# A split-precision self-attention block: exponentials stationary in groups of 256 queries, changed to v stationary with 512 queries streamed

## The chip, the cores and the metric

The kernel runs on one core of a Trainium2 chip. The metric is the device time of one execution in microseconds, the median of several runs. Engines are named as the profile names them: PE is TensorE (its weight loads are PEld), DVE is VectorE, ACT is ScalarE, POOL is GpSimd, SP is SyncE. POOL and SP also issue DMAs here, each in the order of its own queue.

## What is computed

```python
# x (4, 64, 64, 256), Wq and Wk (256, 128), Wv (256, 256); N = 64 * 64 = 4096
q = einsum('bwhc,cd->bwhd', x, Wq) + bq
k = einsum('bwhc,cd->bwhd', x, Wk) + bk
v = einsum('bwhc,cd->bwhd', x, Wv) + bv
pq, pk, pv = (t.reshape(B, -1, N) for t in (q, k, v))     # (4, 128, N), (4, 128, N), (4, 256, N)
energy = einsum('bcn,bcm->bnm', pq, pk)                   # (4, N, N)
attention = softmax(energy, axis=-1)
out = einsum('bcm,bnm->bcn', pv, attention).reshape(x.shape)
return gamma * out + x
```

The reshape is not a transpose: the flat memory of q is read anew as 128 rows of 4096. For each of the four images, 4096 queries n meet 4096 keys m; the weights are normalised over the keys, and 256 rows of v are summed with them.

## The kernel before

**Three forms of each operand.** The matrix unit is fed in a shorter float type (fp32r). To keep float32 accuracy, each operand is split into a rounded upper part h, a remainder l and a combination d, and a product of two float32 matrices is made of three products of forms: h by h and l by l into one accumulator, d by d into another or ahead of the two. For the energies, the product of the third forms comes first (`cross`, products at L322), ScalarE scales it in place in PSUM (L337), the products of the other two forms are added (`energy`, L322 too), and ScalarE takes the exponential (L347). Of each tile of exponentials x, ScalarE makes h (`upper`, L356), and VectorE makes l (L362) and d (L365) (`halves`).

**Tiling.** 128 partitions hold keys. An image has 16 groups of NB = 256 queries, and a group has NU = 8 steps of four key tiles of 128. So an image has 128 steps. In a step, `cross` and `energy` make 12 products with k's form stationary and q's form moving 256 columns, each pair of key tiles in one of four PSUM banks named e. `attend` (L405) makes 24 products with the *exponentials'* forms stationary (128 keys by 128 queries) and v's forms moving: into banks a0 and a1 (one for each half of the group's queries) 258 columns, 256 of v and two of ones, which give the sums of the exponentials, and into bank bb 256 columns for d. The order of a step's 24 products is written out (`ORDERS`). Cross runs four steps ahead of attend, energy three.

**Group end.** At a group's last step ScalarE copies a0 and a1 out (L417). `finish` then runs in pieces, one piece at each call of `proceed`, over the next steps: VectorE copies the two sums (L423), takes the reciprocal (L425), multiplies by gamma (L426) and adds bb (L427); ScalarE scales by the reciprocal (L430); TensorE transposes the result (four products, L438, into bank t); VectorE adds x (L442), which SP loaded three steps before the group's end; POOL's queue stores 256 KB (L443). The last group of all goes through `finish_last` (L450 to L487). All sums are kept on the chip and tested once, at the very end, against the range in which the short path is valid; outside it a general path would run, which does not happen with this data.

**Projection.** Before an image's steps, 16 iterations i (with `begin` interleaving the first energies of the image from i = 10 on) load x (L82, SP's queue), transpose it (L122, copied by L128), and make q and k (`qk`, eight records of float32 products at L135, bias by VectorE at L144) and v (L156, bias by ScalarE at L165). `project_qk` stores q as it is (two DMAs of 64 KB, L275) and k's three forms (384 KB, L279) in HBM, on POOL's queue; k's forms are made by L263 (ScalarE) and L266 (VectorE) in a tile f with two buffers. v's forms stay on the chip (`halve_v`, L292 and L296).

**What sets the order.** The schedule is manual: instructions stand on each engine's queue in the order in which the program issues them, and tiles' buffers make the waits. A step of the main loop issues cross, energy with exponential, `load_k` (all three forms of four key tiles, 768 KB, L314, on POOL's queue; three buffers) for the cross of the next step, halves of the next step, then attend. `load_q` (L303, SP's queue) brings q's values once a group, and `halve_q` makes its forms. POOL's queue therefore holds k's loads and the output's stores, SP's holds x and q.

Of the kernel before, what the change touches and what calls it, by code (L numbers as in the profile page):

```python
# [20 lines left out]
def kernel(  # L21
# [36 lines left out]
    nc = tc.nc  # L58
# [114 lines left out]
    NB = 256  # L173
    NJ = NB // P
    NG = N // NB
    NU = NM // 4
    STEPS = NG * NU
    LOOK = 3
    VC = C + 4
# [4 lines left out]

    again = const.tile([P, 1], I32, name="again")
    zs = const.tile([P, 1], F32, name="zs")

    zall = const.tile([P, B * NG, NJ], F32, name="zall")
# [10 lines left out]
    with ExitStack() as fast:  # L199
# [5 lines left out]

        pool("pad", 1).tile([P, 16], F32, name="pad")
        ppool = pool("ppool", 2)
        pool("pad2", 1).tile([P, 112], F32, name="pad2")
        work = pool("work", 2)
        pool("pad3", 1).tile([P, 48], F32, name="pad3")  # L210
        kpool = pool("kpool", 3)
        dram = pool("dram", 2, space=DRAM)
        ps_s = pool("ps_s", 4, space=PSUM)
        ps_o = pool("ps_o", 1, space=PSUM)
        ps_t = pool("ps_t", 1, space=PSUM)


        vh = qkv.tile([P, NM, VC], F32R, tag="vh", name="vh")
        vl = qkv.tile([P, NM, VC], F32R, tag="vl", name="vl")
        vd = qkv.tile([P, NM, C], F32R, tag="vd", name="vd")  # L220
        for t in (vh, vl):
            nc.scalar.copy(t[:, :, C : C + 2], ones[:, : 2 * NM].rearrange("p (m t) -> p m t", t=2))
# [5 lines left out]
        energies = cycle([(ps_s, "e")])  # L228
        outputs = cycle([(ps_o, "a0"), (ps_o, "a1"), (ps_o, "bb"), (ps_t, "t")])
# [11 lines left out]
        def image(b):  # L241
# [13 lines left out]
            for g in range(NG):  # L255
                qd[b, g] = dram.tile([P, NJ, P], F32, tag=f"qd{g}", name=f"qd_{b}_{g}")
            for t in range(NU):
                kf[b, t] = dram.tile([P, 2, 2, 3 * P], F32R, tag=f"kf{t}", name=f"kf_{b}_{t}")

        def halved(f, x):  # L260

            h = f[:, :, 0, :]
            nc.scalar.activation(h, x, AF.Identity, scale=UPPER / 64)  # L263
            yield
            for j, s, op in ((1, -64.0, ALU.add), (2, 64.0 * (1.0 + E), ALU.subtract)):
                nc.vector.scalar_tensor_tensor(  # L266
                    f[:, :, j, :], h.bitcast(F32), s, x, ALU.mult, op
                )
            yield

        def project_qk(b, i):
            images[b].qk(i)
            x = now["qk"]
            for s in range(2):
                nc.gpsimd.dma_start(qd[b, i // 2 + NG // 2 * s][:, i % 2, :], x[:, s, :C2])  # L275
            f = kpool.tile([P, 2, 3, P], F32R, tag="f", name=f"f_{b}_{i}", bufs=2)
            for _ in halved(f, x[:, :, C2:]):
                pass
            nc.gpsimd.dma_start(kf[b, i // 2][:, i % 2], f.rearrange("p s j d -> p s (j d)"))  # L279
# [8 lines left out]
        def halve_v(b, i):  # L288
            v4 = units.pop((b, "v4", i))
            m = slice(2 * i, 2 * i + 2)  # L290
            h = vh[:, m, :C]
            nc.scalar.activation(h, v4, AF.Identity, scale=UPPER * E)  # L292
            yield

            for t, f in ((vl, 1.0 / E), (vd, 1.0 / E + 1.0)):
                nc.vector.scalar_tensor_tensor(  # L296
                    t[:, m, :C], h.bitcast(F32), -f, v4, ALU.mult, ALU.add
                )
            yield

        def load_q(b, g):
            t = work.tile([P, NJ, P], F32, tag="qr", name=f"qr_{b}_{g}", bufs=1)
            nc.sync.dma_start(t, qd[b, g])  # L303
            loads[b, "qr", g] = t

        def halve_q(b, g):
            t = work.tile([P, 3, NJ, P], F32R, tag="q", name=f"q_{b}_{g}")
            loads[b, "q", g] = t
            yield from halved(t.rearrange("p f j d -> p j f d"), loads.pop((b, "qr", g)))

        def load_k(b, u):
            if u < STEPS:
                t = kpool.tile([P, 4, 3, P], F32R, tag="k", name=f"k_{b}_{u}")
                nc.gpsimd.dma_start(t.rearrange("p (i s) f d -> p i s (f d)", s=2), kf[b, u % NU])  # L314
                loads[b, "k", u] = t

        def chunk(b, u, k, f, first):

            g, t = divmod(u, NU)
            q, kt, e = loads[b, "q", g], loads[b, "k", u], units[b, "e", u, k]  # L320
            for i in range(2):
                nc.tensor.matmul(  # L322
                    e[:, i],
                    kt[:, 2 * k + i, f, :],
                    q[:, f],
                    start=first and i == 0,
                    stop=(f == 1),
                    skip_group_check=True,
                )

        def cross(b, u, k):
# [3 lines left out]
            e = units[b, "e", u, k] = ps_s.tile([P, 2, NJ, P], F32, tag="e", name=f"e_{b}_{u}_{k}")  # L335
            chunk(b, u, k, 2, True)
            nc.scalar.mul(e, e, -1.0 / (1.0 + E))  # L337

        def energy(b, u, k):
# [3 lines left out]
            for f in range(2):  # L343
                chunk(b, u, k, f, False)
            if k == 0:
                units[b, u] = ppool.tile([P, 4, NB], F32, tag="x", name=f"x_{b}_{u}", bufs=3)
            nc.scalar.activation(  # L347
                units[b, u][:, 2 * k : 2 * k + 2, :],
                units.pop((b, "e", u, k)).rearrange("p i j d -> p i (j d)"),
                AF.Exp,  # L350
                scale=(1.0 + E) / E,
            )

        def upper(b, u):
            h = ppool.tile([P, 4, NB], F32R, tag="h", name=f"h_{b}_{u}", bufs=3)
# [3 lines left out]
        def halves(b, u):  # L359
            x, h = units[b, u]  # L360
            l = ppool.tile([P, 4, NB], F32R, tag="l", name=f"l_{b}_{u}")
            nc.vector.tensor_tensor(l, x, h.bitcast(F32), ALU.subtract)  # L362

            d = ppool.tile([P, 4, NB], F32R, tag="d", name=f"d_{b}_{u}")
            nc.vector.scalar_tensor_tensor(  # L365
                d, h.bitcast(F32), 1.0 + E, x, ALU.mult, ALU.subtract
            )
            units[b, u] = h, l, d

        ORDERS = (
            ("13564072", "14325076"),
            ("41256307", "41763502"),
            ("26147053", "35601472"),
            ("41236075", "57104632"),
            ("10436572", "10726543"),
            ("57164203", "34250167"),
            ("35042176", "65341027"),
            ("35210467", "15347062"),  # L380
        )

        def order(f, b, g, t):
            return "01234567" if f == 2 else ORDERS[t][f]

        def attend(b, u):

            g, t = divmod(u, NU)
            if t == 0:
                now["acc"] = [  # L390
                    ps_o.tile([P, C + 2], F32, tag=f"a{j}", name=f"a{j}_{b}_{g}")
                    for j in range(NJ)
                ]
                now["bb"] = ps_o.tile([P, NJ, C], F32, tag="bb", name=f"bb_{b}_{g}")
            h, l, d = units[b, u]
            acc, bb = now["acc"], now["bb"]
            begun = set()
            for f, (left, right) in enumerate(((h, vh), (l, vl), (d, vd))):
                for n, x in enumerate(order(f, b, g, t)):
                    j, i = divmod(int(x), 4)  # L400
# [315 lines left out]
```

## Time and profile before

| what | value |
| --- | --- |
| runs shown, median of 3 | 2455.34 us (2453.41 to 2458.25) |
| profiled execution: its time / its span | 2454.75 us / 2452.9 us |
| granted clock of TensorE in that execution | 0.999 |
| DMA: bytes moved, mean rate | 498.92 MB, 203 GB/s |
| POOL's queue (q0): share of 16 DMA engines | 59.5% |
| chain that ended last: PE / DMA | 91% / 4% |
| products of the energies (L322), busy | 794.7 us in 6144 |
| products of attend (L405), busy, three groups | 569.7, 568.9 and 553.0 us in 4096 each |

The profile is of one execution; its span is the time between its first and last recorded instruction, 1.85 us less than the time of that execution. Busy time of an engine is the union of its instructions' times, so overlapping products do not add up. In the groups of instructions a row gives line, engine, operation, output and inputs (buffer numbers left out), shape, count, then busy time and mean duration of one, then the engine's idle time just before them with what ended most of it. Mean durations of pipelined products overlap (a product of 256 columns lasts 0.278 us, and the next starts 0.113 us after it), so that costs are read from distances of starts, not from durations. In a row of the windows stand: the window, its length, busy time and number of instructions of PE, PEld, DVE, ACT and POOL, the granted clock, the busy share of the DMA engines, and GB/s.

### The profile page before, as it was taken

What the parts mean: (1) busy time and instruction counts of PE and PEld (TensorE: products, weight loads), DVE (VectorE), ACT (ScalarE), POOL (GpSimd) and SP (SyncE); (2) the same over time, 40 slices, a digit from 0 to 9 for tenths busy, and PEclk for the clock granted to TensorE, in tenths of its full rate; (3) what the DMA queues carried; (4) which work ended last, traced back from release to release, by engine and by line L of the source; (5) the groups of instructions that cost most, each with busy time, mean ns of one, the idle gap of its engine ahead of it and who ended that gap; (6) DMA issues with size and microseconds to landing.
All of it is one profiled execution on the core that took longest, in us unless ns stands there. A gap on an engine that the chain in (4) does not pass through costs nothing.

```text
span 2452.9 us, 50094 instructions
## 1 busy us (share of the span) xinstructions
PE 2429.7 (99%) x19988; PEld 2394.9 (98%) x19988; DVE 1523.2 (62%) x1806; ACT 1799.7 (73%) x3201; POOL 424.3 (17%) x781
## 2 busy tenths in 40 slices
PE   9999999999999999999999999999999999999998
PEld 8999999999899999999989999999998999999998
DVE  5666666656665666666566666666566666666665
ACT  5777777777677777777667777777766777777775
POOL 4211111111411111111141111111114111111110
PEclk9999999999999999999999999999999999999999
DMA  7666666665766666666477666666647666666663
GB/s 234 207 207 207 205 211 198 211 207 162 235 204 204 207 207 211 203 203 209 149 241 216 203 205 212 204 212 202 206 146 245 212 207 203 208 205 203 209 205 114
DMA packets 137408, 498.92 MB, mean 203 GB/s; under 512 B 15536, under 2 KB 57264, under 8 KB 137168
## 3 DMA queue, kind: packets, MB, share of 16 engines
q0 software_dynamic: 92320, 453.17, 59.5%
q1 hardware_dynamic: 44304, 42.22, 5.5%
q8 instruction: 160, 2.62, 0.4%
q14 instruction: 80, 0.66, 0.1%
q10 hardware_dynamic: 544, 0.26, 0.0%
HBM read 445.25 MB, written 50.33 MB: 202 GB/s over the span
## 4 chain that ended last, share of the span: by engine, by line
PE 91%; DMA 4%; issue 2%; ACT 1%; DVE 1%; POOL 1%; SPq 0%; POOLq 0%; DVEq 0%; ACTq 0%
PE a L405 38%; PE e L322 28%; PE bb L405 18%; DMA k<-kf 3%; PE qk L135 3%; PE v L156 2%; PE ot L438 1%; DMA kf<-f 1%; PE xt L122 1%; ACT v L165 0%; DVE qks L144 0%; DVE f L266 0%; ACT f L263 0%; DMA x<-in_x_dram 0%; ACT vh L292 0%
## 5 line engine op out<-in xcount | busy, mean ns | idle before, releaser
L337 ACT ACTIVATE e<-e 128x512 f32<-128x512 f32 x1024 | 549.6, 580 | 507.7 <-PE e L322 507.6
L362 DVE TENSOR_TENSOR l<-x,h 128x1024 fp32r<-128x1024 f32 x512 | 626.2, 1223 | 452.1 <-ACT x L347 436.3
L322 PE MATMUL e<-q,k 128*128 128x256 f32 x6144 | 794.7, 278 | 11.6 <-DMA k<-kf 10.2
L322 PEld LDWEIGHTS e<-q,k 128*128 128x128 f32 x6144 | 738.7, 188 | 16.4 <-issue 11.0
L347 ACT ACTIVATE x<-e 128x512 f32<-128x512 f32 x1024 | 621.9, 608 | 5.5 <-issue 5.5
L365 DVE SCALAR_TENSOR_TENSOR d<-h,x 128x1024 fp32r<-128x1024 f32 x512 | 624.0, 1219 | 0.0
L405 PE MATMUL a<-vh,h 128*128 128x258 f32 x4096 | 569.7, 281 | 0.0
L405 PE MATMUL a<-vl,l 128*128 128x258 f32 x4096 | 568.9, 281 | 0.0
L405 PE MATMUL bb<-vd,d 128*128 128x256 f32 x4096 | 553.0, 277 | 0.0
L356 ACT ACTIVATE h<-x 128x1024 fp32r<-128x1024 f32 x512 | 548.4, 1071 | 0.1
L314 POOL DMA_DIRECT2D k<-kf x512 | 274.2, 535 | 1579.7 <-PE e L322 1554.6
L405 PEld LDWEIGHTS a<-vl,l 128*128 128x128 f32 x4096 | 522.0, 189 | 0.0
L405 PEld LDWEIGHTS a<-vh,h 128*128 128x128 f32 x4096 | 519.4, 189 | 0.0
L405 PEld LDWEIGHTS bb<-vd,d 128*128 128x128 f32 x4096 | 510.0, 188 | 0.0
L442 DVE TENSOR_TENSOR x<-x,ot 128x512 f32<-128x512 f32 x63 | 43.3, 687 | 185.8 <-PE ot L438 185.8
L135 PE MATMUL qk<-wqk_sb,xts 128*128 128x256 f32 x512 | 121.0, 379 | 0.0
L156 PE MATMUL v<-xts,wv_sb 128*128 128x256 f32 x512 | 120.3, 379 | 0.0
L156 PEld LDWEIGHTS v<-xts,wv_sb 128*128 128x128 f32 x512 | 97.3, 190 | 13.2
L423 DVE COPY zall<-o 128x2 f32<-128x2 f32 x63 | 10.7, 170 | 160.2 <-ACT o L417 160.2
L135 PEld LDWEIGHTS qk<-wqk_sb,xts 128*128 128x128 f32 x512 | 92.3, 190 | 10.0
L275 POOL DMA_DIRECT2D qd<-qks x128 | 69.2, 549 | 181.1 <-DVE qks L144 171.9
L263 ACT ACTIVATE f<-qks 128x256 fp32r<-128x256 f32 x64 | 26.7, 418 | 74.9 <-DVE qks L144 69.5
(57 smaller groups left out, 788.3 us busy)
## 6 DMA issues: line engine op xcount, KB each, us to landing
k<-kf POOLq DMA_DIRECT2D x512, 768.0 KB, 4.6
x<-in_x_dram SPq DMA_DIRECT2D x128, 256.0 KB, 3.9
kf<-f POOLq DMA_DIRECT2D x64, 384.0 KB, 3.7
out_dram<-x POOLq DMA_DIRECT2D x63, 256.0 KB, 2.5
qd<-qks POOLq DMA_DIRECT2D x128, 64.0 KB, 2.7
qr<-qd SPq DMA_DIRECT2D x64, 128.0 KB, 3.6
wv_sb<-in_L_conv_Wv_dram POOLq DMA_DIRECT2D x1, 256.0 KB, 7.3
out_dram<-x SPq DMA_DIRECT2D x1, 256.0 KB, 3.7
```

The lines of the kernel that those rows point to most:

```text
L135: nc.tensor.matmul(qk[:, s, :], self.xt[i][:, k, s, :], wqk_sb[:, k, :], start=(k == 0), stop=(k == KC - 1),)
L156: nc.tensor.matmul(vp[:, eh, :], wv_sb[:, k, eh * P : (eh + 1) * P], self.xt[i][:, k].rearrange("p s a -> p (s a)"), start=(k == 0), stop= ...
L275: nc.gpsimd.dma_start(qd[b, i // 2 + NG // 2 * s][:, i % 2, :], x[:, s, :C2])
L314: nc.gpsimd.dma_start(t.rearrange("p (i s) f d -> p i s (f d)", s=2), kf[b, u % NU])
L322: nc.tensor.matmul(e[:, i], kt[:, 2 * k + i, f, :], q[:, f], start=first and i == 0, stop=(f == 1), skip_group_check=True,)
L337: nc.scalar.mul(e, e, -1.0 / (1.0 + E))
L347: nc.scalar.activation(units[b, u][:, 2 * k : 2 * k + 2, :], units.pop((b, "e", u, k)).rearrange("p i j d -> p i (j d)"), AF.Exp, scale=(1 ...
L356: nc.scalar.activation(h, units[b, u], AF.Identity, scale=UPPER)
L362: nc.vector.tensor_tensor(l, x, h.bitcast(F32), ALU.subtract)
L365: nc.vector.scalar_tensor_tensor(d, h.bitcast(F32), 1.0 + E, x, ALU.mult, ALU.subtract)
L405: nc.tensor.matmul(out_, left[:, i, j * P : (j + 1) * P], right[:, m, : out_.shape[1]], start=(t == 0 and bank not in begun), stop=(t == N ...
L442: nc.vector.tensor_tensor(xr, xr, tp, ALU.add)
```

## The change

- A group is 512 queries (8 groups an image), a step two key tiles (16 steps a group); there are still 128 steps an image.
- `attend` is turned round: v's forms are stationary (128 keys by 128 of the 256 rows of v), the exponentials' forms move 512 columns. It is called once for each half j of v's rows, six products each, j = 0 between cross and energy, j = 1 after halves. A step has 18 products of 512 columns: two in cross, four in energy, twelve in attend. Accumulators are a0, a1 and b0, b1, a bank each; an e bank holds one key tile by 512 queries.
- The ones columns go. VectorE adds each x to a running sum s in `halves`, and adds its two halves at the group's last step; one float32 product with a matrix of ones puts the sum over the partitions into all of them, in bank b0 (`sums`).
- The result comes out with v's rows on the partitions, so there are no transposes. ScalarE empties the four banks with gamma as scale (`emptied`) and copies the sums; VectorE takes the reciprocal of 128x512, adds the two parts and multiplies. x is no longer loaded for this: a DMA on POOL's queue adds x from HBM into the result's tile, and a second one, behind it, stores 512 KB. One row of the reciprocals is stored (SP's queue) for the range test at the end.
- q's forms are made in the projection together with k's, in one tile f of twice the size, and all of them are stored in HBM (three DMAs an iteration, as before, but 768 KB in place of 512). `load_q` loads the three forms, on POOL's queue. `load_k` loads two key tiles (384 KB, five buffers), two steps before cross uses them.

```diff
-    NB = 256
+    NB = 512
-    NU = NM // 4
-    LOOK = 3
+    NU = NM // 2
+    LOOK = 2
...
-        kpool = pool("kpool", 3)
+        kpool = pool("kpool", 5)
...
+        def project_qk(b, i):
+            images[b].qk(i)
+            qk = now["qk"]
+            f = ppool.tile([P, 2, 3, 2 * C2], F32R, tag="ld", name=f"f_{b}_{i}")
...
+                nc.gpsimd.dma_start(qd[b, i // NJ + NG // 2 * s][:, :, i % NJ, :], f[:, s, :, :C2])
+            nc.gpsimd.dma_start(kf[b, i], f[:, :, :, C2:])
...
         def load_q(b, g):
+            t = work.tile([P, 3, NB], F32R, tag="q", name=f"q_{b}_{g}")
+            nc.gpsimd.dma_start(t, qd[b, g].rearrange("p f j d -> p f (j d)"))
...
         def load_k(b, u):
             if u < STEPS:
+                t = kpool.tile([P, 2, 3, P], F32R, tag="k", name=f"k_{b}_{u}")
+                nc.gpsimd.dma_start(t, kf[b, u % NU])
...
         def halves(b, u):
...
+            if u % NU:
+                s = now["s"]
+                nc.vector.tensor_tensor(s, s, x, ALU.add)
...
+            if u % NU == NU - 1:
+                nc.vector.tensor_tensor(s[:, 0, :], s[:, 0, :], s[:, 1, :], ALU.add)
+                now["sum"] = s[:, 0, :]
...
+        def attend(b, u, j, order=(0, 1, 2)):
...
+            for f in order:
+                to = now["ab"[f == 2], j]
+                for i in range(2):
                     nc.tensor.matmul(
+                        to,
+                        (vh, vl, vd)[f][:, t + NU * i, j * P : (j + 1) * P],
+                        units[b, u][f][:, i, :],
...
+        def emptied(b, g, j):
...
+            for c, scale in enumerate((gam1, gam)):
+                nc.scalar.activation(
+                    now["o"][:, c, j, :], now["ab"[c], j], AF.Identity, scale=scale
+                )
...
+        def sums(b, g, pool, tag):
+            zp = pool.tile([P, NB], F32, tag=tag, name=f"z_{b}_{g}")
+            nc.tensor.matmul(zp, ones, now["sum"], start=True, stop=True)
+            r = work.tile([P, NB], F32, tag="r", name=f"r_{b}_{g}", bufs=1)
+            return zp, r
...
+        def finish(b, g, o):
+            zp, r = sums(b, g, ps_o, "b0")
+            nc.scalar.copy(r, zp)
             yield
+            nc.vector.reciprocal(r, r)
+            nc.sync.dma_start(zd[b * NG + g : b * NG + g + 1, :], r[0:1, :])
             yield
+            nc.vector.tensor_tensor(o[:, 0], o[:, 0], o[:, 1], ALU.add)
             yield
+            nc.vector.tensor_tensor(
+                o[:, 0], o[:, 0], r.unsqueeze(1).to_broadcast([P, 2, NB]), ALU.mult
+            )
+            nc.gpsimd.dma_start(o[:, 0], xg[b, g], accum_op=ALU.add)
+            nc.gpsimd.dma_start(og[b, g], o[:, 0])
...
+                cross(b, u + LOOK + 1)
+                if not final:
+                    attend(b, u, 0)
+                    if t == NU - 1:
+                        emptied(b, g, 0)
+                energy(b, u + LOOK)
+                next(beside, None)
+                upper(b, u + LOOK)
+                load_k(b, u + LOOK + 3)
+                halves(b, u + 1)
...
+                attend(b, u, 1)
+                if t == NU - 1:
+                    emptied(b, g, 1)
+                    start(finish(b, g, now["o"]))
+                else:
+                    proceed()
```

In the changed kernel's own line numbers: cross's products stand at L306 and its scaling at L307, energy's products at L321 and the exponential at L324, h at L330, s at L339, l at L344, d at L346, the last addition of s at L350, attend's products at L363, the evictions at L377, the product of ones at L384, the copy at L390, reciprocal L392, addition L395, product L397, the adding DMA L400, the store L401, q's load L288, k's load L294.

## The prediction, made before the changed kernel ran

> **What bounds the kernel now.** I read the page's engine totals first, then the timeline of a steady step, the groups of instructions (shapes kept apart), the DMA issues, and the span by windows.
>
> ```profile
> PE 2429.7 (99%) x19988; PEld 2394.9 (98%) x19988; DVE 1523.2 (62%) x1806; ACT 1799.7 (73%) x3201; POOL 424.3 (17%) x781
> ```
>
> TensorE is never idle, and its weight loads (PEld) are as full as its products. One step of the timeline:
>
> ```profile
> 408.70 1.44 PEld L322 LDWEIGHTS e<-q,k 128*128 128x128 f32 x12
> 408.81 1.52 PE L322 MATMUL e<-q,k 128*128 128x256 f32 x12
> ...
> 410.18 1.11 PE L405 MATMUL a<-vh,h 128*128 128x258 f32 x8
> ...
> 411.12 1.10 PE L405 MATMUL a<-vl,l 128*128 128x258 f32 x8
> ...
> 412.07 1.08 PE L405 MATMUL bb<-vd,d 128*128 128x256 f32 x8
> ...
> 412.98 1.52 PE L322 MATMUL e<-q,k 128*128 128x256 f32 x12
> ```
>
> From 408.81 to 412.98 is a step of 36 products: 4.17 us, 116 ns each. Twelve in 1.52 us, the last lasting 0.276, are (1.52-0.276)/11 = 113 ns apart. The projection's products give the other price:
>
> ```profile
> 643.03 1.89 PE L135 MATMUL qk<-wqk_sb,xts 128*128 128x256 f32 x8
> ```
>
> Four float32 products of 256 columns leave eight records, (1.89-0.379)/7 = 216 ns apart, each with its own 128-wide weight load: it is the nearest row for a product that streams about twice as long as the steady ones beside one weight load. These pay 226 to 236 ns for two of 256, and their weight loads start as closely (113) as they do; at 216 ns half of that time is to spare.
>
> The Trainium skill, page TensorE: Matmul & The Clock Gate, section Back-to-back issue gap, states two rules for 512 columns: N/2.4 + 2.5 ns when isolated (216, as this row), and about 131 ns sustained. The row bears out the first; what the second would make of the time is a rival below.
>
> The other engines and the transfers:
>
> ```profile
> L362 DVE TENSOR_TENSOR l<-x,h 128x1024 fp32r<-128x1024 f32 x512 | 626.2, 1223 | 452.1 <-ACT x L347 436.3 <-ACT h L356 5.9 <-issue 1.8
> ...
> L337 ACT ACTIVATE e<-e 128x512 f32<-128x512 f32 x1024 | 549.6, 580 | 507.7 <-PE e L322 507.6
> ...
> L425 DVE RECIPROCAL r<-zall 128x2 f32<-128x2 f32 x63 | 10.5, 166 | 2.2
> ...
> L464 DVE RECIPROCAL r<-zall 128x1 f32<-128x1 f32 x2 | 0.3, 164 | 0.1
> ```
>
> ```profile
> k<-kf POOLq DMA_DIRECT2D x512, 768.0 KB, 4.6
> x<-in_x_dram SPq DMA_DIRECT2D x128, 256.0 KB, 3.9
> kf<-f POOLq DMA_DIRECT2D x64, 384.0 KB, 3.7
> out_dram<-x POOLq DMA_DIRECT2D x63, 256.0 KB, 2.5
> ```
>
> ```profile
> 621.00:690.00 69.00, 66.14 (x361) 58.74 (x360) 44.75 (x80) 46.09 (x96) 29.31 (x55) 1.00 0.80 247
> ...
> 1194.43:1802.85 608.42, 606.20 (x4994) 597.58 (x4993) 380.22 (x448) 449.45 (x802) 105.07 (x192) 1.00 0.66 205
> ```
>
> The second window is one image, from one eviction of sums (L417) to the same one an image later: 608.4 us. Sixteen groups of eight steps are 16 x 33.9 = 542.4 (33.9 is the usual distance of two L417; 0.45 of it are the transposes); the projection is the other 66.0, with DMA engines 80% busy. Four images are 2433.6; start and end are the other 19 of the span of 2452.9. That execution took 2454.75 us, 0.6 under the median of the runs.
>
> **The sum, part by part.** All per image, with 8 groups of 16 steps.
>
> 1. *Products.* A step is 18 products of 512 columns: 18 x 0.216 = 3.89 us, a group 62.2, against 67.8 for two old groups: -44.8. Bounds: 0.215 (the closest of L135) and 0.227 (twice 113 ns), 495 to 523 us an image; I take the row of the same streaming time, 497.6.
>
> 2. *VectorE.* Back-to-back operations of 1024 elements start 1.14 us apart (408.14 l, 409.28 d). A step has three (s, l, d): 3.42 of 3.89, idle 0.47. A group's end adds a 512-element add and reciprocal (0.6 each, as the 512-element rows), an add and a product of 1024 (1.14 each), and one s less. d is ready 2 us before its products; the lag adds up to about 1.6 and is worked off: nothing. The reciprocal of 512 is not in the trace: from 1 to 2 elements it grows by 2 ns (164, 166), as the product L465 and L426 does (159, 161), which at 512 elements takes 0.69; 2 ns an element would make it 1.2. I take 0.7. What goes from here and ScalarE (q's halving, 0.75 and 0.43 an old group, x's addition) was beside the products: nothing.
>
> 3. *ScalarE.* Two muls and two exponentials start 0.48 apart, what follows h 0.94 (410.27 x, 410.75 h, 411.69 x), and h now waits for the x just before it (0.15): 3.05 of 3.89. At a group's end four evictions with a pointer scale (0.57 apart: 0.48 plus the 0.1 that L430 shows over L417) and the copy of zp queue behind the exponentials. From the last step's start I lay: a0 1.6, b0 2.1, exponentials 2.7 and 3.2, h 3.8, a1 4.8, b1 5.4, copy 5.9 to 6.5. TensorE does zp (float32, 512 columns: 4 x 0.216 = 0.86) until 4.75, and reaches b0, which zp holds, at 6.05: 0.5 of waiting. So 1.4 a group, 11.2; bounds 0.9 and 2.0.
>
> 4. *POOL's queue.* L400 and L401 are new there: the accumulate waits for VectorE's product, the output waits for the accumulate's landing, and k's load for unit 8 of the next group is queued behind both; TensorE needs that k at step 5. From the last step's start: x of unit 2 is there at 8.8; s, l, d (3.42) 12.2; add 13.4; s, l, d of unit 3 16.8; product 18.0. Accumulate landed: +4.6, by the row k<-kf, which reads and writes as many bytes as an accumulate of 512 KB that reads two sources and writes one. Bounds 3.3 (one pass, out_dram's 2.5 and 0.75 for the second half of the bytes) and 7.0 (three passes). Output issued 0.7, k 2.7 (half of k's bytes, like the quickest kf<-f) plus 1.1 behind 512 KB of output (behind 256 KB k took 5.1, elsewhere 4.6): 4.5. It lands at 27.2; step 5 is due at 9.2 + 4 x 3.89 = 24.75. TensorE waits 2.5 (bounds 0 and 4.9), in 7 groups of 8: 17.5.
>
> 5. *Projection.* Products unchanged. f holds q's and k's forms in pieces of 512 B: 768 KB an i instead of 512, and POOL issues three DMAs of some 3 us together (0.54 for 128 pieces, 0.69 for 256 by rows L279 and L443, so 0.85 twice and 1.3) of 3.89. f has two buffers, and its next writer waits for the landing; at 80% DMA before, near 95% now, I give 4 us. In three of four images the accumulate blocks POOL while f waits: about 4.7, so 3.5 on the mean. Together +7.5; bounds 0 and 16. Against this k's loads are halved (402 MB become 201) and the steady DMA share falls; k's old wait at the first step (2.5 us, at 686.8) gives way to l's for f's landing, of the same size. SP keeps x's loads, two ahead, behind one store of r: nothing.
>
> 6. *Ends.* The start is the same. After the last product there are fewer steps (no transposes), but zp stands before it: 0, bounds -3 and +3 in all.
>
> Image: 497.6 + 11.2 + 17.5 + 66.0 + 7.5 = 599.8, 8.6 less; four are -34.4. 2454.75 - 34.4 = 2420.3; with 0.6 for the median 2421 us.
>
> **The rivals.**
>
> *k is in time.* If the accumulate takes 3.3 and k isn't held up, wait 4 is 0: 497.6 + 11.2 + 66 + 3 = 577.8, 2333 us. For it: the quick landings (out_dram 2.5). Against: the landing is waited for in the queue.
>
> *The accumulate is slow* (the other side): at 7.0 the wait is 4.9 in 7 groups, 34.3, and the projection's 7.5 becomes 14: 623 an image, 2514 us. It turns slower than before once the landing passes 5.8 us: (608.4-599.8)/7 = 1.2 over 4.6. For it: no accumulating DMA is in the trace, and x's plain 256 KB take 3.9.
>
> *The reciprocal runs several cycles an element.* Each us more moves the product at 18.0, and k: from 1.9 us (3.5 ns an element) the kernel is slower than before. At eight times the 1.05 ns of the other rows ((1223-687)/512) it takes 4.3: the product moves by 3.7, d is late in three steps (3.0 in all), and k by 3 more: 630 an image, 2543 us. The rows (166 against 164) speak against it. The Trainium skill, page VectorE: DVE Perf Modes, section First, the fixed hardware budget, says that reciprocal is an iterative divide with a repeat count of 8. Eight cycles an element would be 8 ns between those two rows; they show 2.
>
> *The change doesn't do what it says*: 512 columns cost two of 256, 0.227. Group 65.2, waits of 1.5: 617 an image, 2490 us. Against: 216 ns in row L135.
>
> *TensorE sustains far less than 216 ns.* Then VectorE bounds: 16 x 3.42 + 2.3 = 57 a group, 530 an image, 2140 us. Against: steady products of 256 columns are 113 apart, never under half of 216. The page named first is where this rule stands.
>
> **How the numbers follow.** Forecast 2421 (2350 to 2449): 0.50. k in time: 0.22. Within 0.2% (about what a measurement of this kernel can tell from no change), 2450 to 2460: 0.05. Slow accumulate 0.13, slow reciprocal 0.06, no gain by 512 columns 0.03; sustained rule 0.01. Faster 0.73, same 0.05, slower 0.22. The range leaves out what is below 2320 and above 2495.
>
> **What would show it.** Products L363 216 ns apart; steps 3.89; one wait of TensorE a group for k at L306, near 2.5, and one near 0.5 for ACT r; the accumulate landing in 4.6; L392 at 0.7; the projection near 73 us. I am wrong if L306 never waits for k, or if VectorE, not POOL, is what TensorE waits for.

## The result and the profile after

The changed kernel takes 2737.85 us (median of 4, 2733.12 to 2742.61) against 2455.0 us before: ratio 1.115, 95% interval 1.1126 to 1.1175. It is slower by 11.5%; 2421 was forecast, and the range ended at 2495. The profiled execution took 2742.61 us, its span is 2740.7.

The engine totals, the groups and the DMA issues in question, of the changed kernel's page:

```profile
PE 2481.9 (91%) x10580; PEld 2015.3 (74%) x10580; DVE 2143.2 (78%) x1966; ACT 1846.0 (67%) x3039; POOL 500.3 (18%) x812
...
L306 PE MATMUL e<-q,k 128*128 128x512 f32 x1024 | 344.5, 419 | 178.3 <-DMA k<-kf 178.3
...
kf<-f POOLq DMA_DIRECT2D x64, 384.0 KB, 4.4
...
o<-in_x_dram POOLq DMA_DIRECT2D x31, 512.0 KB, 5.8
out_dram<-o POOLq DMA_DIRECT2D x31, 512.0 KB, 3.2
```

and from its groups by shape:

```profile
L392 DVE RECIPROCAL r<-r 128x512 f32<-128x512 f32 x31 | 103.7, 3346 | 0.0
```

TensorE went from 99% to 91%: it waits, 178.3 us of it at L306 for k. The accumulate lands in 5.8 us, the reciprocal takes 3.35. One group end on TensorE's timeline (start, length, operation, and the idle time ahead of it):

```profile
248.10 0.62 PE L363 MATMUL a<-ld,vl 128*128 128x512 f32 x2
248.57 0.61 PE L363 MATMUL b<-ld,vd 128*128 128x512 f32 x2
255.47 1.19 PE L306 MATMUL e<-q,k 128*128 128x512 f32 x2 [6.29 <-DMA k<-kf]
256.46 1.05 PE L363 MATMUL a<-h,vh 128*128 128x512 f32 x2
257.31 1.05 PE L363 MATMUL a<-ld,vl 128*128 128x512 f32 x2
258.17 1.05 PE L363 MATMUL b<-ld,vd 128*128 128x512 f32 x2
259.02 1.23 PE L321 MATMUL e<-q,k 128*128 128x512 f32 x4
260.09 0.62 PE L363 MATMUL a<-h,vh 128*128 128x512 f32 x2
260.55 0.62 PE L363 MATMUL a<-ld,vl 128*128 128x512 f32 x2
```

Two things are to be seen. The wait is 6.29 us. And the pairs behind it are 0.85 us apart (256.46 to 257.31) where usual pairs are 0.45 to 0.46 apart: products at 0.427 us until about 259.4, which costs 2 us more. In the window from 250 to 260 us the granted clock (the column behind POOL's) is 0.66; in the ten us before and behind it is 1.00:

```profile
250.00:260.00 10.00, 4.53 (x12) 3.66 (x13) 2.90 (x3) 1.25 (x3) 2.97 (x6) 0.66 0.89 288
```

The POOL queue of the same time:

```profile
243.27 1.10 POOL L400 DMA_DIRECT2D o<-in_x_dram  x1 [11.14 <-DVE o L397]
249.52 0.73 POOL L401 DMA_DIRECT2D out_dram<-o  x1 [5.15 <-DMA o<-in_x_dram]
250.15 1.75 POOL L294 DMA_DIRECT2D k<-kf  x3
```

POOL stood for 11.1 us at the accumulate, waiting for VectorE's product, then 5.15 for its landing, with three loads of k behind it. The first of them landed at 255.3, and TensorE goes on at 255.47.

**Where 317 us went** (2737.85 - 2421), each term from distances of starts in this trace, against the forecast's own:

| term | forecast | measured | difference, all images |
| --- | --- | --- | --- |
| product of 512 columns | 0.216 us | 0.227 us | 9216 x 0.011 = +101 |
| wait for k, 28 groups | 2.5 us | 6.37 us (178.3/28) | +108 |
| products at half speed after it | none | 2.08 us a group | +58 |
| image change with projection | 73.5 us | 89 to 95 us | some +54 |
| wait for bank b0 | 0.5 us | 0.38 us | -4 |

A group is thus 16 x 4.08 + 0.86 (product of ones) + 0.38 + 6.37 + 2.08 = 75.0; products of ones stand 75.1 us apart. The image change is a remainder: what an image (679.4, 681.9 and 685.3 us from the first product of ones of one image to that of the next) takes beyond eight groups of 66.5 and seven waits of 8.4 (6.37 and 2.08).

### The profile page after: what moved, and what is told of

Read it like the earlier page. It is cut to its first block, busy times and chain, and to the rows that moved or that the text cites. A ratio compares the mean times of both kernels' runs of the same rounds, so it can differ in the third digit from the quotient of the medians.

```text
span 2740.7 us, 30274 instructions
## 1 busy us (share of the span) xinstructions
PE 2481.9 (91%) x10580; PEld 2015.3 (74%) x10580; DVE 2143.2 (78%) x1966; ACT 1846.0 (67%) x3039; POOL 500.3 (18%) x812
## 2 busy tenths in 40 slices
DMA packets 211724, 330.00 MB, mean 120 GB/s; under 512 B 14191, under 2 KB 129391, under 8 KB 211566
## 4 chain that ended last, share of the span: by engine, by line
PE 57%; issue 11%; DMA 11%; ACT 9%; DVE 9%; POOL 2%; POOLq 0%; SPq 0%; ACTq 0%; DVEq 0%
PE a L363 24%; PE b L363 13%; PE e L321 12%; PE e L306 7%; DMA k<-kf 6%; DMA kf<-f 5%; ACT o L377 3%; DVE s L339 2%; ACT x L324 2%; DVE ld L346 2%; ACT h L330 2%; DVE o L397 1%; DVE o L395 1%; POOL o L400 1%; ACT v L165 1%
## 5 line engine op out<-in xcount | busy, mean ns | idle before, releaser
L339 DVE TENSOR_TENSOR s<-s,x 128x1024 f32<-128x1024 f32 x480 | 585.5, 1220 | 398.8 <-ACT x L324 398.2
L324 ACT ACTIVATE x<-e 128x512 f32<-128x512 f32 x960 | 523.0, 597 | 468.9 <-PE e L321 468.8
L307 ACT ACTIVATE e<-e 128x512 f32<-128x512 f32 x1024 | 545.6, 567 | 191.9 <-PE e L306 191.8
L363 PE MATMUL a<-ld,vl 128*128 128x512 f32 x2048 | 645.4, 397 | 10.6 <-DVE ld L344 10.6
L363 PE MATMUL b<-ld,vd 128*128 128x512 f32 x2048 | 651.5, 400 | 3.7 <-DVE ld L346 0.8
L363 PE MATMUL a<-h,vh 128*128 128x512 f32 x2048 | 645.8, 397 | 1.1 <-ACT v L165 1.1
L344 DVE TENSOR_TENSOR ld<-x,h 128x1024 fp32r<-128x1024 f32 x480 | 584.9, 1218 | 4.5 <-DMA kf<-f 4.5
L346 DVE SCALAR_TENSOR_TENSOR ld<-h,x 128x1024 fp32r<-128x1024 f32 x480 | 584.9, 1219 | 0.0
L321 PE MATMUL e<-q,k 128*128 128x512 f32 x2048 | 561.9, 397 | 1.0 <-ACT e L307 1.0
L294 POOL DMA_DIRECT2D k<-kf x512 | 292.1, 592 | 1482.1 <-PE e L321 1450.4
L330 ACT ACTIVATE h<-x 128x1024 fp32r<-128x1024 f32 x480 | 509.5, 1062 | 14.9
L306 PE MATMUL e<-q,k 128*128 128x512 f32 x1024 | 344.5, 419 | 178.3 <-DMA k<-kf 178.3
L363 PEld LDWEIGHTS b<-ld,vd 128*128 128x128 f32 x2048 | 388.6, 192 | 104.9 <-ACT r L390 14.7
L363 PEld LDWEIGHTS a<-ld,vl 128*128 128x128 f32 x2048 | 393.2, 192 | 96.1 <-DVE ld L344 12.4
L321 PEld LDWEIGHTS e<-q,k 128*128 128x128 f32 x2048 | 396.2, 194 | 88.4 <-ACT e L307 2.3
L363 PEld LDWEIGHTS a<-h,vh 128*128 128x128 f32 x2048 | 393.6, 192 | 86.6 <-ACT v L165 1.9
L306 PEld LDWEIGHTS e<-q,k 128*128 128x128 f32 x1024 | 195.7, 195 | 238.4 <-issue 196.4
L135 PE MATMUL qk<-wqk_sb,xts 128*128 128x256 f32 x512 | 133.9, 408 | 2.5 <-ACT xts L128 2.3
L156 PE MATMUL v<-xts,wv_sb 128*128 128x256 f32 x512 | 122.4, 384 | 0.0
```

What stands on the lines that cost most here:

```text
L135: nc.tensor.matmul(qk[:, s, :], self.xt[i][:, k, s, :], wqk_sb[:, k, :], start=(k == 0), stop=(k == KC - 1),)
L156: nc.tensor.matmul(vp[:, eh, :], wv_sb[:, k, eh * P : (eh + 1) * P], self.xt[i][:, k].rearrange("p s a -> p (s a)"), start=(k == 0), stop= ...
L294: nc.gpsimd.dma_start(t, kf[b, u % NU])
L306: nc.tensor.matmul(e, *forms(b, u, i, 2), start=True, stop=False, skip_group_check=True)
L321: nc.tensor.matmul(e, *forms(b, u, i, f), start=False, stop=(f == 1), skip_group_check=True)
L324: nc.scalar.activation(x[:, i, :], e, AF.Exp, scale=(1.0 + E) / E)
```

## Experiments

Up to the first of the two layout kernels each kernel is the changed kernel with one change of its own; the later ones build on each other, as their texts say. Where no number of runs is given, there was one; the four runs of the changed kernel spread over 9.5 us, so that differences of some 10 us between single runs are weak. The kernel before took 2455 to 2458 us in the same sets.

### The result's store on SP's queue

```diff
-            nc.gpsimd.dma_start(og[b, g], o[:, 0])
+            (nc.sync if g < NG - 1 else nc.gpsimd).dma_start(og[b, g], o[:, 0])
```

> Only the store of a group's result (L401) moves from POOL's queue to SP's, in the first seven groups of an image; the accumulate (L400) stays on POOL's. Theory (POOL's queue holds k): in the changed kernel POOL issued the accumulate at 243.27, waited for its landing until 249.52 and issued the next k at 250.15. Without the store that k goes out at 244.4, 5.75 us earlier, so the wait of 6.3 us at L306 falls under 1 us, and the half-speed products after it (0.427 apart, some 2.2 us more a group) go too: 28 groups x (5.75+2.2) = 223, so about 2515 us. Rival (the DMA engines are what is slow: k lands late beside the accumulate and the store, wherever it is issued): waits of 3 us and more stay, over 2600 us. Rival (VectorE is the bound): no change, 2738.

Measured: 2542.69 us. The waits of TensorE:

```profile
PE e L306 <- DMA k<-kf: 31.1, 28, 1.8
```

178.3 became 31.1, groups 75.1 became 68.0 us, and no product behind these 28 waits (at most 1.8 us each) ran at half speed. 195 us went by moving one DMA (223 were expected), with every transfer still made and the accumulate as slow as before (5.80 us). So it was the order of the queue, not the DMA engines. What is left (1.1 a group) is that POOL still stands at the accumulate until the product is there; in the group looked at (accumulate issued at 238.41) the next k was issued 0.7 us after it and landed in 6.0.

### The reciprocal left out

```diff
-            nc.vector.reciprocal(r, r)
+            nc.vector.tensor_scalar(r, r, 0.0, 1.0, ALU.mult, ALU.add)
```

> The reciprocal of 128x512 (3.35 us) is replaced by a VectorE operation that writes 1.0 (about 0.69 us), so the result is not normalised: this part of the computation is left out. Queue theory: the product and with it the accumulate come 2.65 us earlier, the wait for k at L306 falls from 6.3 to about 3.7, and if the products behind a wait of 3.7 still run at half speed the time falls by 28 x 2.65 plus some 8 at the three image changes, to about 2655; if not, by 60 more, to about 2595. Rival (the start of the accumulate does not set the wait): wait unchanged at 6.3 and the time within 10 us of 2738.

Measured: 2700.9 us; the wait for k is 140.8 us in 28, 5.0 each: 1.3 less, not 2.65. VectorE's timeline tells why:

```profile
229.48 0.42 DVE L392 TENSOR_SCALAR r<-r 128x512 f32<-128x512 f32 x1
231.18 1.23 DVE L339 TENSOR_TENSOR s<-s,x 128x1024 f32<-128x1024 f32 x1 [1.27 <-ACT x L324]
```

Without the reciprocal VectorE is early and waits 1.27 us for the next x, so the product comes only 1.5 us earlier after the product of ones (239.13 - 226.32 = 12.8, against 241.46 - 227.15 = 14.3). The wait fell by 1.3, nearly as much as the product came earlier: the start of the accumulate does set the wait, and the reciprocal moves that start by half of what it takes. Neither 2655 nor 2595 came; the products behind the waits of 5.0 still ran at half speed.

### Products of 256 columns in attend

```diff
-                    nc.tensor.matmul(
-                        to,
...
-                        units[b, u][f][:, i, :],
...
+                    for n in range(2):
+                        nc.tensor.matmul(
+                            to[:, n * 256 : (n + 1) * 256],
...
+                            units[b, u][f][:, i, n * 256 : (n + 1) * 256],
```

> Each of attend's products of 512 columns becomes two of 256 with the same stationary operand: 24 a step in place of 12, the rest unchanged. Theory: these products are paid by the column (0.227 for 512, 0.113 for 256, with no gain from a longer one), so steps stay at 4.08 us and the time at 2738 within 10. Rival (512 columns save something per product, as the float32 rows at 0.216 suggested): two of 256 cost more than one of 512, 0.24 or more, and 512 steps x 12 x 0.013 are 80 us or more. Rival (512 columns are slowed by their length): the time falls below 2700.

Measured: 2806.42 us, 69 more. TensorE's timeline of a step, four products of 256 in a row where two of 512 were:

```profile
801.68 0.63 PE L364 MATMUL a<-h,vh 128*128 128x256 f32 x4
802.14 0.64 PE L364 MATMUL a<-ld,vl 128*128 128x256 f32 x4
802.62 0.64 PE L364 MATMUL b<-ld,vd 128*128 128x256 f32 x4
803.10 1.09 PE L321 MATMUL e<-q,k 128*128 128x512 f32 x4
804.03 0.63 PE L364 MATMUL a<-h,vh 128*128 128x256 f32 x4
```

Four take 0.46 to 0.48, 117 to 120 ns each, and the 512-column products of the energies rose with them (803.10 to 804.03: 233 each). The first rival holds in kind, at 69 us in place of 80: in this kernel 512 columns do save 3 to 6% over two of 256. Against the kernel *before*, whose 256 columns stood 113 apart, 512 columns at 227 save nothing. Why 256 columns cost 117 to 120 here and 113 there is not settled.

### The store of the reciprocals' row behind the result

> Only the store of one row of the reciprocals (L393, SP's queue) moves from behind the reciprocal to behind the result's store in the program. In the changed kernel x's loads for the next image stood behind it on SP's queue until 683.87, TensorE waited 5.6 us for x, and the products after it ran at half speed (some 2.3 us). Theory: both go at three image changes, 3 x 7.9 = 24 us, about 2714. Rival (the projection is set by the landing of k's and q's forms, and the time is waited for there instead): less than 6 us, 2732 to 2738.

The edit moves the line with `zd` behind the store of the result. Measured: 2721.46 us, 16 less; the wait for x, 12.3 us in 3, fell to 1.5. In the changed kernel's queue this is plain:

```profile
683.87 0.21 SPq L393 DMA_DIRECT2D zd<-r  x1
684.18 22.61 SPq L82 DMA_DIRECT2D x<-in_x_dram  x8
```

x's loads could not start before the reciprocal, because a store of 2 KB that needs it stood ahead of them. Two thirds of the 24 expected came; TensorE's waits at L135 and L156 for ScalarE and VectorE rose from 2.3 to 8.4 us.

### x added by VectorE, all of a group's end on SP

```diff
             nc.vector.tensor_tensor(o[:, 0], o[:, 0], o[:, 1], ALU.add)
+            nc.sync.dma_start(o[:, 1], xg[b, g])
...
-            nc.gpsimd.dma_start(o[:, 0], xg[b, g], accum_op=ALU.add)
-            nc.gpsimd.dma_start(og[b, g], o[:, 0])
+            nc.sync.dma_start(zd[b * NG + g : b * NG + g + 1, :], r[0:1, :])
+            yield
+            nc.vector.tensor_tensor(o[:, 0], o[:, 0], o[:, 1], ALU.add)
+            nc.sync.dma_start(og[b, g], o[:, 0])
```

> The accumulate is taken out in every group: SP loads x into the half of o that the addition has freed, VectorE adds it one step after the product, and SP stores the result; the store of the reciprocals' row stands behind the product. POOL's queue then holds only k and q (and the projection's stores). Queue theory: the wait for k at L306 goes altogether (178 us in 28 waits in the changed kernel, 31 with the store alone moved) with the half-speed products after it, groups are 16 x 4.08 + 0.86 + 0.38 = 66.5 in place of 75.1 us, 28 x 8.6 = 241; at the image changes 16 as with the late store of the row and up to 9 more. About 2475 us. Rival (VectorE, with 61.9 us of work in 66.5, is late now): waits of L363 for VectorE, groups of 68 or more, 2515 and over. Rival (k's landing is slow beside q's 768 KB whatever the queue): waits of about 1 stay, 2500.

Measured: 2528.53 us. The waits of TensorE, the costliest first:

```profile
PE xt L122 <- DMA x<-in_x_dram: 48.6, 7, 8.7
...
PE b L363 <- DVE ld L346: 6.6, 33, 0.5
```

No wait for k is left in the whole list, and groups are 67.2 us. But the miss against 2475 has the same cause in another queue: SP now waits for VectorE in the group's end, and at an image change x's loads stand behind it, 48.6 us and half speed after. The image change went from 156 to 158 us (products of ones before and behind it) to 159 to 162.

### The projection's forms: layout, then three buffers

```diff
-            f = ppool.tile([P, 2, 3, 2 * C2], F32R, tag="ld", name=f"f_{b}_{i}")
+            fs = [
+                ppool.tile([P, 2, 3, P], F32R, tag="hx"[c], name=f"f{c}_{b}_{i}", bufs=3)
+                for c in range(2)
+            ]
...
-                nc.gpsimd.dma_start(qd[b, i // NJ + NG // 2 * s][:, :, i % NJ, :], f[:, s, :, :C2])
-            nc.gpsimd.dma_start(kf[b, i], f[:, :, :, C2:])
+                nc.gpsimd.dma_start(qd[b, i // NJ + NG // 2 * s][:, i % NJ], fs[0][:, s])
+            nc.gpsimd.dma_start(kf[b, i], fs[1])
```

The first of the two kernels has this layout in the old tile of two buffers. The second also splits that tile in two and puts them where h and x lie, so it changes more than the number of buffers.

> The changed kernel with q's and k's forms laid out one after the other in the tile f and in HBM, so that the projection's stores and q's loads run over 1.5 KB and 3 KB at a time in place of 512 B; ScalarE and VectorE make the forms in pieces of 256 elements in place of 512; bytes, queues and buffers stay. Theory (512 B pieces make the projection's DMAs slow): projection's 88 us an image fall to about 80, 2738 - 4 x 8 = about 2705. Rival (bytes, or the two buffers with the wait for the accumulate, set it): within 10 us of 2738.

> As the kernel with forms laid out one after the other, and q's and k's forms in two tiles with three buffers each (those of h and x, idle in the projection), so that ScalarE's L257 waits less for the landing of k's forms (71 us in the changed kernel) and the first l and d of an image do not share buffers with them. Theory (the two buffers bind): the projection falls to about 73 us an image, 2738 - 4 x 15 = about 2678. Rival (POOL's queue, held by the accumulate and by the issue of three stores, or the DMA engines, full, set it): the gain over the two-buffer layout is under 10 us.

Measured: 2720.02 and 2708.82 us. With two buffers, packets under 2 KB fell from 129391 to 47471, k's forms land in 3.9 in place of 4.4 us, and ScalarE's wait for them fell from 71.3 to 44.7; image changes (between products of ones) are 151 us with two buffers and 148 to 149 with three. The layout brought 18 us of the 33 expected, and the second kernel 29 of 60; the 11 between the two single runs are little more than the spread of one kernel's runs, but image changes, too, are 2 to 3 us shorter. So the projection was bound by more than its buffers.

### Both together, and SP's DMAs a step later

> Both together: x added by VectorE with SP's queue for x, row and result, and forms laid out one after the other with three buffers. Theory: 2475 less what the three buffers bring (60), about 2415 us, 1.7 per cent under the kernel before: of two ones columns that go (0.09 a step, 46 us), 29 us are given back to the product of ones and 12 to the wait for bank b0, so the gain is what the projection and the transposes leave. Rival (the projection with 768 KB an iteration stays at 80 us and more): 2440 to 2475, no faster than before.

Measured: 2506.92 us, 92 more than the theory and beyond the rival's 2475 too; waits for x of 46.4 us remain, as in the kernel with x on VectorE, and neither the theory nor the rival had counted them.

The next one issues each of SP's three DMAs at least one step behind the VectorE operation that they need; the one after it moves the product of ones.

```diff
             nc.vector.tensor_tensor(o[:, 0], o[:, 0], o[:, 1], ALU.add)
-            nc.sync.dma_start(o[:, 1], xg[b, g])
             yield
+            nc.sync.dma_start(o[:, 1], xg[b, g])
...
-            nc.sync.dma_start(zd[b * NG + g : b * NG + g + 1, :], r[0:1, :])
+            yield
             yield
             nc.vector.tensor_tensor(o[:, 0], o[:, 0], o[:, 1], ALU.add)
+            yield
             nc.sync.dma_start(og[b, g], o[:, 0])
+            nc.sync.dma_start(zd[b * NG + g : b * NG + g + 1, :], r[0:1, :])
```

> The kernel with x added by VectorE and three buffers for the forms, with SP's three DMAs of a group's end each issued at least one step after the VectorE operation that they wait for, so that SP's queue never stands still in front of x's loads for the next image. In the kernel with both changes TensorE waited 7.8 and 9.1 us for x at an image change, and the products after it ran at half speed for about 3.5 us. Theory: these go, 3 x 20 = 60, about 2446 us, 0.4 per cent under the kernel before. Rival (the image change is set by POOL's queue or by VectorE, which has the reciprocal there, and the time is waited for elsewhere): 2480 to 2507.

Measured: 2466.38 us (6 runs), ratio to before 1.0038 (1.0026 to 1.0051): 40 us less, not 60. Waits for x are 17.0 us, at most 3.4.

> As the kernel before it in this set, with the product of ones moved from the group's end to the middle of the next step, into bank b1 in place of b0, which ScalarE has emptied by then and which the next group needs half a step later. In the changed kernel attend's first product into b0 stood 0.49 and the next 0.34 behind its predecessor, 0.38 us lost a group. Theory: these go, 28 x 0.38 = 10.5, about 2436 us. Rival (the copy, now ahead of a step's exponentials on ScalarE, or b1 late, costs as much): within 3 us of the kernel without it, or slower.

Measured: 2481.09 us, 1.0098 (1.008 to 1.0116): slower by 15 us than without. The wait for b0 went, but the product of ones now waited 0.3 us for b1, and d came 0.35 and 0.44 us late in two steps of a group, where it was 0.16 late in one: VectorE now waits 0.55 us for the copy in front of its reciprocal, and its lag has to be worked off. The rival's time held, and with it one of its two causes (b1 late, 0.3 us); the late d was in neither the theory nor the rival.

### bfloat16 in attend

```diff
-            qkv.tile([P, NM, C], F32R, tag=name, name=name) for name in ("vh", "vl", "vd")
+            qkv.tile([P, NM, C], BF16, tag=name, name=name) for name in ("vh", "vl", "vd")
...
-            h = ppool.tile([P, 2, NB], F32R, tag="h", name=f"h_{b}_{u}", bufs=3)
+            h = ppool.tile([P, 2, NB], BF16, tag="h", name=f"h_{b}_{u}", bufs=3)
...
-            ld = ppool.tile([P, 2, 2, NB], F32R, tag="ld", name=f"ld_{b}_{u}")
+            ld = ppool.tile([P, 2, 2, NB], BF16, tag="ld", name=f"ld_{b}_{u}")
```

> As the first kernel of this set, with the exponentials' and v's forms kept as bfloat16, so that attend's twelve products a step are bfloat16 (the precision is given up, the kinds and sizes of products stay). Theory (the type sets the price: fp32r streams 512 columns in 0.227, float32 a pass of as many in 0.216): attend's products stand 0.216 apart, cross's and energy's stay at 0.227, a step is 3.95, 68 us less in all, about 2378. Rival (accumulation, weight loads or the length set it): 0.227 everywhere, within 10 us of the first kernel of this set.

Measured: 2434.94 us, 31 less than its base. On TensorE's timeline:

```profile
400.53 0.61 PE L369 MATMUL a<-h,vh 128*128 128x512 bf16 x2
400.98 0.59 PE L369 MATMUL a<-ld,vl 128*128 128x512 bf16 x2
401.41 0.59 PE L369 MATMUL b<-ld,vd 128*128 128x512 bf16 x2
401.65 1.28 PE L327 MATMUL e<-q,k 128*128 128x512 f32 x4
402.77 0.61 PE L369 MATMUL a<-h,vh 128*128 128x512 bf16 x2
```

Two bfloat16 products are 0.43 apart (400.98 to 401.41), 215 to 216 ns each, in the place where fp32r took 227, with the same sizes and the same accumulation. The weight loads did not stay the same: their records last 98 ns, and 188 in the base.

```profile
L369 PEld LDWEIGHTS <-vl 128*128 128x128 bf16 x2048 | 200.6, 98 | 249.4 <-issue 9.1
```

So this run alone does not part the type from the length of the weight load. The projection's float32 products do speak for the type: they stand 216 ns apart beside weight loads of 190 ns and more. A run with fp32r products and short weight loads is missing. Half of the gain is given back: in the steps shown the six products of the energies take 1.40 us in place of 1.36, and the first bfloat16 product behind them is followed after 227 to 229 ns.

### The last group's end behind the projection

```diff
                 project_v(b, i - 1)
-                proceed()
...
             nc.scalar.copy(r, zp)
-            yield
+            for _ in range(1 if g < NG - 1 else 5):
+                yield
```

> As the kernel whose SP DMAs come a step late, with the end of an image's last group (reciprocal, addition, product, x, store) moved behind the projection of the next image, into its steps from the fifth on. In that kernel VectorE, with the forms of q as well as k, had 3.4 us of work in a projection iteration of 3.9, and the group's end (3.35 + 3 x 1.14) pushed it back, so that SP's load of x into o, which waits for the addition, still held x's loads for the image: waits of 3.4 and 2.6 us for x, and products at half speed after them (granted clock 0.83 in two stretches of 10 us). Theory: these 6 us of waits and about 3.5 of half speed go, with the smaller waits for VectorE, 10 to 12 an image change, three changes: about 2432 us, 1 per cent under the kernel before. Rival (the projection is set by the landing of its stores or by ScalarE's L165, whose release of the banks TensorE waits for): 2455 to 2466. Rival (the reciprocal between the first steps makes l and d late there): 2445 to 2455.

Measured: 2444.99 us (5 runs), ratio to before 0.9953 (0.994 to 0.9967): 0.5% faster than the kernel before, and 21 us faster than its base. The windows of an image change, in columns the window, its length, then PE, PEld, DVE, ACT and POOL busy, the granted clock, the DMA share and GB/s; first without the step, then with it:

```profile
625.00:635.00 10.00, 6.64 (x27) 5.47 (x26) 8.51 (x16) 5.11 (x12) 2.75 (x6) 0.83 0.93 289
...
645.00:655.00 10.00, 7.63 (x32) 6.51 (x33) 5.84 (x14) 5.18 (x12) 4.40 (x9) 0.83 1.12 364
```

```profile
625.00:635.00 10.00, 10.00 (x54) 8.83 (x53) 8.07 (x18) 6.93 (x17) 4.22 (x8) 1.00 1.00 299
...
645.00:655.00 10.00, 10.00 (x51) 8.68 (x51) 7.78 (x18) 7.36 (x18) 4.25 (x8) 1.00 1.19 383
```

TensorE is full through the projection, with VectorE at 8 of 10 and the DMA engines full. An image change fell from 144 to 146 us to 139.5 to 139.8. 13 us of the 34 that were expected did not come. What TensorE still waits for is at an image's first steps, where l and d are late (9.5 and 4.1 us in all, and 5.3 for ScalarE and the last q and k), with a granted clock of 0.83 from 675 to 685 us.

## Why the prediction was wrong, by its own steps

Two steps failed above all. Step 1 (products) mis-sized the price of a product (0.216 us against 0.227 measured), and so lost 101 of the 179 us (4 x 44.8) that the products were to gain. Step 4 (POOL's queue) had the right wait at the right place, but 2.5 us long where 6.37 were measured, and no term for the products at half speed behind it; this made the loss. Step 5 (projection) missed another 54. Neither sign of being wrong that the prediction named came: L306 waits for k, and it is not VectorE that TensorE waits for.

1. **Products: wrong by size.** The step took the float32 projection's 216 ns "as the row of the same streaming time", though the kernel's own fp32r row gave 2 x 113 and was in its bounds. The trace has 227. That the type makes the difference is supported by the float32 rows and the bfloat16 run, with weight loads not fully parted from it. So a step is 4.08 us against 4.17 before, and not 3.89. The 0.09 lie in the sixteen products with ones columns: 258 columns stand 118.7 apart there, 256 stand 113 in the energies, and 16 x 5.7 ns are 0.09. Whether the two columns cause it is not shown, for 256 columns without them took 117 to 120 in the run with products of 256. The Trainium skill, page TensorE: Matmul & The Clock Gate, section Back-to-back issue gap, with N/2.4 + 2.5 ns gives 216 for 512 columns: float32 and bfloat16 agree (215 to 216), fp32r does not (227). Its other rule, 131 ns sustained, is in no row.
2. **VectorE: right that it is no bound, wrong in the reciprocal.** It takes 3.35 us, not 0.7: the two rows 164 and 166 ns for one and two elements say nothing of 512. The Trainium skill, page VectorE: DVE Perf Modes, section First, the fixed hardware budget, names a repeat count of 8; the prediction made 8 ns an element of it, and the measured (3346-164)/512 = 6.2 ns lie nearer to that than to the 2 that the step tried as its dearer case.
3. **ScalarE and bank b0: right.** 0.38 against 0.5, the product of ones 0.858 against 0.86.
4. **POOL's queue: right mechanism, wrong size.** k was late behind the accumulate and the store, in 28 groups, as forecast. Counted from the start of the product of ones (3.9 us into the forecast's last step), on the mean of these groups, VectorE's product ended after 15.5 us (forecast 18.0 - 3.9 = 14.1: the reciprocal), the store was issued 6.7 later (4.6: the accumulate's landing, 5.8, and its issue), and k landed 6.0 behind that (4.5). TensorE wanted it 22.0 after the product of ones (20.9), because its steps were longer. So 1.4 + 2.1 + 1.5 - 1.2 = 3.8 us were added to 2.5. What the step left out is the price of a long wait: 2 us of products at half speed. A wait as long as the forecast's 2.5 stood in the trace before, for k too, and cost nothing more (2.49 us, no slow products).
5. **Projection: wrong in two places.** "SP keeps x's loads, two ahead, behind one store of r: nothing" failed: the 2 KB store waits for the reciprocal, and x waits behind it; moving it brought 16 us. And VectorE's work there (forms of q too, 3.4 us of 3.89) was not summed, nor the group's end that falls into it; taking that end out brought 21 us. The layout of the forms brought 18. These runs stand on different bases, so that the parts need not add up to the 54.
6. **The rivals.** Slow accumulate (2514), slow reciprocal (2543) and no gain by 512 columns (2490) had chances of 0.13, 0.06 and 0.03, as if at most one would come. All three came in kind: 2421 + 93 + 122 + 69 = 2705, within 33 of the result. That it comes so near is luck: two of the sizes were too high (a landing of 7.0 where 5.8 was measured, a reciprocal of 4.3 where it took 3.35, of which only half reached the queue), and the half speed and most of the image change were in none of them. Nor do they simply add: longer steps give k more time, by 1.2 us here.

That the order of the queues made the loss is shown by taking it away: with the store alone off POOL's queue 195 us went, and without the places where a DMA queue waits for something in front of another transfer's turn, with the forms in a new layout and the last group's end moved, the same products take 2445 us, a little less than the kernel before. The 101 us of the products stay in that kernel; what is shown for them is the distance of 227 ns, and its cause only in part.

## What to carry to other kernels

A DMA that waits, on a queue that also feeds TensorE, is paid by everything behind it: list per queue what each entry waits for before moving one there, and issue it a step after its operand is ready. Take a product's price from rows of the same type. When several rivals lengthen the same chain, let the range hold them together; they don't exclude each other.

## What the runs showed of the hardware

- A product of 512 columns stands 227 ns ahead of the next in fp32r, 215 to 216 in bfloat16, and 858 in float32 (the product of ones).
- Behind the 28 waits for k (6.37 us each) TensorE's products ran at 0.427 us for 512 columns, for about 2 us in excess, and also behind those of 5.0 without the reciprocal; behind waits of up to 1.8 us for k they did not. In the group shown TensorE is idle from 249.18 to 255.47, and the trace's record of the granted clock has the half from 252.49 to 259.31.
- The length of one wait does not decide. In each of the fourteen traces all changes of the granted clock stand at multiples of 3.41 us from each other (within 0.01). Cut into these stretches, by the recorded busy time of TensorE, all 281 stretches at full clock with more than 2.0 us idle are followed by half clock, none of the 9688 with less than 1.68 us is, and 19 of the 33 between are. So a wait of 2.55 us for x at an image change (SP's DMAs a step later), all within one stretch, was followed by half clock; one of 2.49 in the kernel before, 1.1 in one stretch and 1.4 in the next, was not. The Trainium skill, page TensorE: Matmul & The Clock Gate, section What's actually happening, says that the clock is halved after an idle window of about 3.4 us: the length of the window agrees, but here some two of the 3.4 us idle were enough.
- A reciprocal of 128x512 takes 3.35 us where an addition takes 0.69.
- An accumulate of 512 KB lands in 5.8 us, a store of the same in 3.2, and a plain load of the same x, on SP's queue in the kernel with x added by VectorE, in 4.0.
